# Differential attention: the second value sum in two pieces, and the side work of a unit's nine phases dealt out anew

## The chip, the cores and the metric

The kernel runs on one core of a Trainium2 chip. The engines of that core are named as in the profile: PE multiplies matrices (PEld is its weight load), DVE and POOL work on vectors, ACT computes functions and copies, SP issues DMAs. The metric is the time of one execution on the device in microseconds (us), lower is better. Before the change the median of three runs is 1141.25 us (1139.06 to 1142.85).

## The reference

Four blocks follow one another, each with a layer norm ahead of it and a residual sum behind it: attention A, a mixture of eight small experts, attention B, and the same experts again. The change touches attention A alone. For 2 sequences of 1024 rows of width 512 it computes, cut to its core:

```python
q = rotary((x @ Wq).reshape(b, t, 2 * H, D)); k = rotary((x @ Wk).reshape(b, t, 2 * H, D))   # H = 16, D = 16
v = (x @ Wv).reshape(b, t, H, 2, D)
attn1 = softmax(mask(q1 @ k1.T * scale)) @ concat(v1, v2)      # first map of each head
attn2 = softmax(mask(q2 @ k2.T * scale)) @ concat(v1, v2)      # second map of each head
attn = irfft((rfft(attn1) - lam * rfft(attn2)) * filt)         # along the rows
attn = attn * rsqrt(mean(attn ** 2) + eps) * rms_weight * (1 - LAMBDA_INIT)
out = attn.reshape(b, t, 512) @ Wout
```

The mask is causal. Each head has two score maps that share their values; the second map is taken off the first, weighted by `lam`. The filter along the rows is linear, so it comes after the sum over values.

## The kernel before

Attention A is worked off in 16 units (`NU`): a unit `n` is one sequence and two heads. The 1024 rows of queries are eight tiles of 128, `j` = 0 to 7; because of the mask, tile `j` of queries meets `j + 1` tiles of keys. A unit has nine phases (`NP`), and each phase takes row tiles whose key tiles make up exactly eight: phase 0 is head 0 with tile 7, phase 1 head 1 with tile 7, phase 2 tile 6 of one head and tile 0 of the other, and so on; phase 8 has tile 3 of both heads. Unit `n`'s phase `ph` is step `t = 9 n + ph` of one long loop, whose body writes out the order of instructions for PE, DVE, ACT and POOL by hand. What stands earlier in the body stands earlier in each engine's queue, and every queue is worked off in order.

A row tile goes through three steps `t`, `t + 1`, `t + 2`:

- step `t`, `scores` (L434, its matmuls L475 and L488): PE writes two maps of 128 x 1024 scores; DVE takes the row minimum of each (`minima`, L502 and L510); ACT takes the exponentials and their sums (`exponentials`, L519).
- step `t + 1`, `share` (L539), `divide` (L545, L547) and `join` (L554): POOL and DVE form a ratio from the two sums, and DVE adds the second map times that ratio to the first. The ratio is two small products on POOL: L539 stands at the start of the step, L547 after DVE's reciprocal.
- step `t + 2`, `transpose` (L578, L580): PE turns the joined map in two halves of four blocks each, and ACT copies them to the tile `dt`. A single PSUM bank serves both halves.

Beside this runs the side work. It is entered ahead of time into lists under a step number. The list `large` holds pieces that need the one PSUM bank `misc` of 512 columns: PE's part stands between the two halves of the transposes, and the eviction by ACT or DVE at the end of the step:

- `project` (L355, L366): queries and keys of the next unit, four pieces of 256 columns; pieces 0 and 1 make half 1 (rows 512 to 1023), pieces 2 and 3 make half 0. After the second piece of a half SP issues a DMA that swaps neighbouring rows into `other` (L371).
- `rotate` (L399 to L401), two steps after that second piece, in the list `middle`, which stands after `divide` in the body: three products and sums of 128 x 512 on POOL, and then the DMAs into `keys` (L403) and, for half 1, `swapped` (L408).
- `project_values` (L379, L387): the value tiles of the next pair of units, one or two row tiles at a time; they overwrite those of two pairs before.
- `weigh` (L605, L617, L618): the sum over values. Four groups of matmuls stand side by side in the columns of PE (32 each), one matmul of each group per round. Part 0 has tiles 7, 6 and 0, part 1 has tiles 5 down to 1. ACT evicts it to `oT`.
- `finish` (L627 to L634): PE turns `oT` back, DVE multiplies by the reciprocal sums and writes `result`.
- `spread_half` (L333): the turned input of the second sequence, in the first six units; its layer norm has pieces on DVE, ACT and POOL (`norm_sums`, `norm_tables`, `norm_scale`).

`fold` (L651 to L654) stands in `rear`, the last list of a step: eight sums and differences on POOL that put a unit's result into the form that the filter needs. It comes at phase 6 of the next unit. `bring` loads the second sequence's turned input over the first one's.

Before the change the phases of a unit hold this side work (W0, W1 the two parts of `weigh`, F0, F1 their `finish`, Q0 to Q3 the pieces of `project`, V a value tile, V2 two of them; X, a piece of `spread_half`, only in the first units):

| phase | 0 | 1 | 2 | 3 | 4 | 5 | 6 | 7 | 8 |
|---|---|---|---|---|---|---|---|---|---|
| `large` | Q1 | X, Q2 | W1 | Q3 | F1, V | X, V2 | W0 | F0, V | X, Q0 |
| POOL | | | rotate half 1 | | | rotate half 0 | fold | | |

Units 6 to 9, where the kernel passes from one sequence to the other, have other steps for their value tiles. These lines of the body give the order that matters for POOL: `share` comes early in a step, `divide` and then `middle` in its middle, `rear` last:

```python
if last:
    divide(*last)
do(middle, t)
```

Of the kernel before, what the change touches and what calls it, by code (L numbers as in the profile page):

```python
# [2 lines left out]

# [1 line left out]

# [6 lines left out]
F32 = mybir.dt.float32  # L12
# [6 lines left out]
P = 128  # L19
# [6 lines left out]
NQ = 4  # L26
# [52 lines left out]
def hybrid_layer_kernel(ctx: ExitStack, tc: tile.TileContext, i: dict, out: bass.AP):  # L79
    nc = tc.nc  # L80
# [66 lines left out]
    with ExitStack() as sa:  # L147
# [8 lines left out]
        with ExitStack() as sp:  # L156
# [6 lines left out]
            work = sp.enter_context(tc.tile_pool(name="work", bufs=2))  # L163
# [3 lines left out]
            def misc(name):  # L167
                return ps_m.tile([P, 512], F32, tag="x", name=name)
# [4 lines left out]
            def spare(name):  # L173

                return ps_s.tile([P, 2, 512], F32, tag="s", name=name)[:, 0, :]
# [54 lines left out]
            def load_others(k):  # L230
# [22 lines left out]
                base=0,  # L253
# [172 lines left out]
            NP = len(PHASES)  # L426
            units = [(b, qt, blk) for b in range(NB) for qt in range(NQ) for blk in range(2)]
            NU = len(units)
            least, sums = {}, {}
            weights, turned = {}, {}  # L430
# [133 lines left out]
            def transpose(n, ph, half):  # L564
# [11 lines left out]
                for k in range(4):  # L576
# [4 lines left out]

            PARTS = [
                (0, 3, [[(0, 7, 0)], [(1, 7, 0)], [(0, 6, 0), (0, 0, P)], [(1, 6, 0), (1, 0, P)]]),
                (
                    3,
                    8,
                    [
                        [(0, 5, 0), (0, 3, P)],  # L590
                        [(1, 5, 0), (1, 3, P)],
                        [(0, 4, 0), (0, 2, P), (0, 1, 2 * P)],
                        [(1, 4, 0), (1, 2, P), (1, 1, 2 * P)],
                    ],
                ),
            ]

            def weigh(bank, c0, n, part):
                _, _, groups = PARTS[part]
                po = bank[:, c0 : c0 + P * (part + 2)]  # L600
                order = [[(h, j, c0, k) for h, j, c0 in g for k in range(j + 1)] for g in groups]
                for blocks in zip(*order):
                    for g, (h, j, c0, k) in enumerate(blocks):
                        dt, at = turned[n, h, j, k]
                        nc.tensor.matmul(  # L605
                            po[32 * g : 32 * g + 32, c0 : c0 + P],
                            vals[n // 2 % 2][:, k, 64 * (n % 2) + 32 * h : 64 * (n % 2) + 32 * h + 32],
                            dt[:, at, :],
                            start=(k == 0),
                            stop=(k == j),  # L610
                            tile_position=(0, 32 * g),
                        )
                yield

                full = P * (part + 1)
                oT = work.tile([P, 3 * P], F32, tag="oT", name=f"oT_{n}_{part}")
                nc.scalar.copy(oT[:, 0:full], po[:, 0:full])  # L617
                nc.scalar.copy(oT[64:P, full : full + P], po[64:P, full : full + P])  # L618
                turned[n, part] = oT

            def finish(bank, c0, n, part):
                oT = turned[n, part]
                lo, hi, _ = PARTS[part]
                tp = bank[:, c0 : c0 + 64 * (hi - lo)]
                full = P * (part + 1)
                for at in range(0, full, P):
                    nc.tensor.transpose(tp[:, at : at + P], oT[:, at : at + P], ident)  # L627
                nc.tensor.transpose(tp[:, full : full + 64], oT[64:P, full : full + P], ident[64:P, 64:P])
                yield
                if part == 0:  # L630
                    results[n] = work.tile([P, JT, 64], F32, tag="result", name=f"result_{n}", bufs=1)
                rec = tally.tile([P, 5, 2], F32, tag="rec", name=f"rec_{n}_{part}")[:, 0 : hi - lo, :]
                nc.vector.reciprocal(rec, sums[n][0][:, 2 * lo : 2 * hi].rearrange("p (r h) -> p r h", h=2))
                nc.vector.tensor_mul(  # L634
                    results[n][:, lo:hi, :].rearrange("p r (h f) -> p r h f", h=2),
                    tp.rearrange("p (r h f) -> p r h f", h=2, f=32),
                    rec[:, :, :, None].to_broadcast([P, hi - lo, 2, 32]),
                )
# [21 lines left out]
            front, small, large, middle, final, rear = {}, {}, {}, {}, {}, {}  # L660

            def at(which, t, what, *args):
                which.setdefault(t, []).append((what, args))
# [8 lines left out]

            for n in range(NU):
                t = n * NP
                for part, (t_sum, t_end) in enumerate(((6, 7), (NP + 2, NP + 4 - (n >= NU - 2)))):
                    at(large, t + t_sum, weigh, P * (part + 2), n, part)
                    at(large, t + t_end, finish, (192, 320)[part], n, part)
                at(rear, t + NP + (3 if n == NU - 1 else 6), fold, n)

            PROJECT = (-1, 0, 1, 3)
            VALUES = {p: [(k, w) for k, w in ((-14, 1), (-13, 2), (-11, 1), (-5, 1), (-4, 2), (-2, 1))] for p in range(1, 8)}
            VALUES[4] = [(-5, 1), (-4, 2), (-2, 1), (0, 1), (4, 1), (5, 2)]
            VALUES[5] = [(-11, 1), (-10, 1), (-9, 1), (-8, 1), (-5, 1), (-4, 2), (-2, 1)]

            SPREAD = [n * NP + k for n in range(6) for k in (1, 5, 8)][1:]
            for j in range(JT):
                t = SPREAD[2 * j]
                at(rear, t - 4, load_x, JT + j)  # L690
# [3 lines left out]
                for half in range(2):  # L694
                    at(large, SPREAD[2 * j + half], spread_half, 256, j, half)
            for half in range(2):
                at(rear, (2 * NQ - 2) * NP + PROJECT[3 - 2 * half], bring, half)
            for k in range(4):
                at(rear, 2 * k + (18 if 0 < k < 3 else 0), load_others, k)
            for u in range(2, 2 * NQ):  # L700
# [3 lines left out]
            for u in range(1, NU):  # L704
                t = (u - 1) * NP
                for piece in range(4):
                    if t + PROJECT[piece] >= 0:
                        at(large, t + PROJECT[piece], project, 256, u, piece)
                    if piece % 2:
                        at(middle, t + PROJECT[piece] + 2, rotate, u, 1 - piece // 2)  # L710
                if u % 2 == 0:
                    j = JT
                    for k, w in VALUES[u // 2]:
                        j -= w
                        at(large, u * NP + k, project_values, w * P, u // 2, j, w)
                    assert j == 0
# [89 lines left out]
            t = (NU - 2) * NP  # L806
# [8 lines left out]
            for n in range(MIXED):  # L815
                f = t + FILTER + 1 + n
# [8 lines left out]
            with tc.manual_schedule(engines=ordered | {mybir.EngineType.Pool}):  # L825
# [18 lines left out]
                for t in range(NU * NP + 6):  # L844
# [22 lines left out]
                    if (NU - 1) * NP <= t < (NU - 1) * NP + EC:  # L867
                        part = wout[:, t - (NU - 1) * NP, :]
# [14 lines left out]
                    begun, c0 = [], 0  # L883
                    for what, (width, *args) in large.pop(t, ()):
                        if t >= NU * NP and width == 512:
                            bank, c0 = spare(f"bank_{t}_{len(begun)}"), 0
                        elif c0 == 0:
                            bank = misc(f"bank_{t}")
# [31 lines left out]
        with ExitStack() as sb:  # L920
            wb = sb.enter_context(tc.tile_pool(name="wb", bufs=1, reuse_waits="tile"))
            work = sb.enter_context(tc.tile_pool(name="workb", bufs=2, reuse_waits="tile"))
# [109 lines left out]
            groups, scales, xns, xTs, hidden, acts = {}, {}, {}, {}, {}, {}  # L1032
# [259 lines left out]
            with tc.manual_schedule(engines=ordered):  # L1292
                for t in range(NTILE + 2):
# [28 lines left out]
                    if mixing:  # L1322

                        n = MIXED + t
# [8 lines left out]
                    turned = MIXED + t - 2 if 0 <= t - 2 < NTILE - MIXED else None  # L1333
# [140 lines left out]
```

## Time and profile before

| | us |
|---|---|
| median of three runs | 1141.25 (1139.06 to 1142.85) |
| profiled execution, first to last instruction | 1142.6 |
| attention A's phases, first to last minimum on DVE | 36 to 705 |
| PE busy | 1067.2 (93%) |
| DVE busy | 930.8 (81%) |
| ACT busy | 766.9 (67%) |
| POOL busy | 438.1 (38%) |

Of the profiled execution the page gives the span of its instructions and no other total; the span lies 1.35 us above the median of the runs. A line of a timeline gives start and duration in us, engine, source line, operation, what is written from what, the shape, and in brackets the idle time of the engine before it and what ended that. A line of the table of stretches gives a stretch of the span, its length, each engine's busy time and its number of instructions, the clock that was granted to PE (1.00 is full), and the share and rate of the DMAs. A busy PE is not a PE at its peak, since matmuls overlap.

### The profile page before, as it was taken

How to read it: one execution, taken by the hardware profiler on the slowest of the kernel's cores; microseconds unless marked ns; L12 is line 12 of the kernel's file. 1: busy time of each engine (PE TensorE's matmuls, PEld its weight loads, DVE VectorE, ACT ScalarE, POOL GpSimd, SP SyncE). 2: the span in 40 equal slices, each digit the busy share in tenths (PEclk: the TensorE clock that was granted, in tenths of full speed). 3: DMA queues.
4: the chain of work that ended last, by engine and by line, in shares of the span. 5: the costliest groups of instructions: out<-in, count | busy, mean ns of one | idle time of the engine just before them, and what ended most of it. 6: DMA issues, size and time to landing. Idle time of an engine off the chain costs nothing.

```text
span 1142.6 us, 23491 instructions
## 1 busy us (share of the span) xinstructions
PE 1067.2 (93%) x8680; PEld 732.3 (64%) x8680; DVE 930.8 (81%) x2046; ACT 766.9 (67%) x2010; POOL 438.1 (38%) x689
## 2 busy tenths in 40 slices
PE   6899999999889999999999979889999999999997
PEld 5777777777677877777777655544555455554554
DVE  5699999999889889889989998577787777758677
ACT  3588988989879889899999877243433433443433
POOL 1246446345345444534535672122323223223300
PEclk9999999999989999999999999889999999999999
DMA  5212222211301101110110521200000000001002
GB/s 176 79 42 67 80 80 66 71 38 52 116 15 39 42 16 38 48 33 25 39 43 16 182 114 39 111 1 1 0 1 1 1 1 1 1 1 37 1 19 92
DMA packets 33345, 52.19 MB, mean 46 GB/s; under 512 B 6480, under 2 KB 11088, under 8 KB 33104
## 3 DMA queue, kind: packets, MB, share of 16 engines
q1 hardware_dynamic: 33072, 50.44, 13.8%
q8 instruction: 69, 1.13, 0.4%
q14 instruction: 44, 0.36, 0.1%
q10 hardware_dynamic: 160, 0.26, 0.1%
HBM read 23.42 MB, written 6.29 MB: 26 GB/s over the span
## 4 chain that ended last, share of the span: by engine, by line
PE 55%; DVE 26%; ACT 11%; issue 5%; POOL 2%; DMA 1%; SPq 0%; DVEq 0%; POOLq 0%; ACTq 0%
DVE least L510 8%; PE s L488 8%; ACT p L519 7%; DVE p L554 6%; PE pq_q L1224 5%; PE py L1287 5%; PE bank L355 4%; PE pq_v L1224 4%; PE dtp L578 4%; PE pq_k L1224 4%; PE z L1028 3%; PE bank L605 3%; DVE least L502 3%; PE hr_f L1092 2%; PE y L978 2%
## 5 line engine op out<-in xcount | busy, mean ns | idle before, releaser
L519 ACT ACTIVATE p<-s,least 128x640 f32<-128x640 f32 (+7 forms) x512 | 378.3, 744 | 41.9 <-DVE least L510 27.9
L510 DVE TENSOR_REDUCE least<-s 128x1 f32<-128x896 f32 (+5 forms) x384 | 244.2, 679 | 35.4 <-PE s L488 35.4
L554 DVE SCALAR_TENSOR_TENSOR p<-p,ratio,p 128x1024 f32<-128x1024 f32 (+7 forms) x256 | 227.0, 922 | 3.5 <-POOL ratio L547 3.4
L578 PE MATMUL dtp<-ident,p 128*128 128x128 f32 x1152 | 184.8, 283 | 14.1 <-ACT dt L580 7.9
L580 ACT COPY dt<-dtp 128x512 f32<-128x512 f32 x288 | 168.9, 586 | 42.9 <-PE dtp L578 39.5
L488 PE MATMUL s<-keys,qk 32*128 32x128 f32 (+3 forms) x1408 | 169.0, 445 | 0.0
L578 PEld LDWEIGHTS dtp<-ident,p 128*128 128x128 f32 x1152 | 128.8, 142 | 58.2 <-ACT dt L580 30.4
L502 DVE TENSOR_REDUCE least<-s 128x1 f32<-128x1024 f32 (+1 forms) x96 | 115.9, 1213 | 26.5 <-PE s L488 26.5
L488 PEld LDWEIGHTS s<-keys,qk 32*128 32x128 f32 x1408 | 94.2, 188 | 49.3 <-issue 43.0
L547 POOL TENSOR_TENSOR ratio<-ratio,inverse 128x2 f32<-128x2 f32 (+1 forms) x144 | 28.1, 195 | 243.0 <-DVE inverse L545 217.9
L539 POOL TENSOR_TENSOR ratio<-sums,neg_lam 128x2 f32<-128x2 f32 (+1 forms) x144 | 73.6, 511 | 117.9 <-ACT p L519 117.6
L355 PE MATMUL bank<-xnT,wqk 128*128 128x256 f32 x472 | 115.8, 389 | 2.8 <-ACT raw L366 1.8
L488 PE MATMUL s<-swapped 32*128 32x128 f32 (+2 forms) x896 | 104.8, 345 | 0.0
L519 ACT ACTIVATION_READ_ACCUMULATOR p<-s,least 128x1 f32 x512 | 104.2, 203 | 0.0
L355 PEld LDWEIGHTS bank<-xnT,wqk 128*128 128x128 f32 x472 | 86.0, 192 | 18.0 <-ACT raw L366 5.6
L488 PEld LDWEIGHTS s<-swapped 32*128 32x128 f32 x896 | 71.0, 185 | 9.5
L475 PE MATMUL s<-eye 128*128 128x256 bf16 (+1 forms) x320 | 60.8, 251 | 16.5 <-ACT p L519 15.5
L605 PE MATMUL bank<-dt,v 128*32 128x128 f32 x2304 | 69.5, 274 | 1.7 <-ACT v L387 0.7
L605 PEld LDWEIGHTS bank<-dt,v 128*32 128x32 f32 x2304 | 60.9, 110 | 8.0 <-ACT v L387 4.4
L400 POOL TENSOR_TENSOR other<-other,rope_a_sb 128x512 f32<-128x512 f32 x30 | 63.0, 2099 | 0.0
L1247 POOL TENSOR_TENSOR qkv_v<-qkv_v,qkv_k 128x512 f32<-128x512 f32 x16 | 20.4, 1274 | 108.5 <-DVE qkv_v L1246 107.4
L379 PE MATMUL bank<-wval,xnT 128*128 128x128 f32 x448 | 60.4, 282 | 0.8
(222 smaller groups left out, 1790.8 us busy)
## 6 DMA issues: line engine op xcount, KB each, us to landing
other<-raw SPq DMA_DIRECT2D x64, 128.0 KB, 2.1
xin<-in_query SPq DMA_DIRECT2D x16, 256.0 KB, 2.9
keys<-qk SPq DMA_DIRECT2D x64, 64.0 KB, 1.9
swapped<-keys SPq DMA_DIRECT2D x32, 128.0 KB, 2.3
x_sb<-in_query SPq DMA_DIRECT2D x16, 256.0 KB, 6.3
out_dram<-x_sb SPq DMA_DIRECT2D x16, 256.0 KB, 2.2
swapped<-qk SPq DMA_DIRECT2D x30, 128.0 KB, 2.3
wqk<-in_w_qk SPq DMA_DIRECT2D x8, 256.0 KB, 2.8
```

What stands on the lines that cost most here:

```text
L355: nc.tensor.matmul(pp, wqk[:, part, c, :], xnT[b, half][:, c, t0 : t0 + 256], start=(c == 0), stop=(c == EC - 1),)
L400: engine.tensor_mul(other, other, rope_a[:, 1, cols])
L488: nc.tensor.matmul(s[mm][:, c0 : c0 + w], q[r0 : r0 + 32, j * P - back : (j + 1) * P - back], k[r0 : r0 + 32, s0 - back : s0 - back + w], ...
L502: nc.vector.tensor_reduce(least[n][:, e[0] : e[-1] + 1 : e[-1] - e[0] or 1, mm], s[mm].rearrange("p (g k) -> p g k", g=g), AX.X, ALU.min,)
L510: nc.vector.tensor_reduce(least[n][:, e, mm : mm + 1], s[mm][:, c0 : c0 + w], AX.X, ALU.min)
L519: nc.scalar.activation(ps[mm][:, c0 : c0 + w], sv, AF.Exp, bias=low, scale=-1.0, accum_out=sums[n][mm][:, e : e + 1],)
L539: nc.gpsimd.tensor_mul(ratio[:, w], first, neg_lam.to_broadcast([P, w.stop]))
L554: nc.vector.scalar_tensor_tensor(ps[0][:, c0 : c0 + w], ps[1][:, c0 : c0 + w], ratio[:, k : k + 1], ps[0][:, c0 : c0 + w], ALU.mult, ALU.add,)
L578: nc.tensor.transpose(tp[:, k * P : (k + 1) * P], d[:, c0 : c0 + P], ident)
L580: nc.scalar.copy(dt[:, 4 * half : 4 * half + 4, :], tp.rearrange("p (k q) -> p k q", k=4))
L605: nc.tensor.matmul(po[32 * g : 32 * g + 32, c0 : c0 + P], vals[n // 2 % 2][:, k, 64 * (n % 2) + 32 * h : 64 * (n % 2) + 32 * h + 32], dt[: ...
L1224: nc.tensor.matmul(pq, hTs[n][:, c, :], win(c, s), start=(c == 0), stop=(c == EC - 1))
```

## The change

Part 1 of `weigh` becomes two pieces. Piece 1 has tiles 5 and 4 (groups of six and five rounds), piece 2 has tiles 3, 2 and 1 (four and five rounds). Because groups of a piece are no longer of one length, the rounds are dealt with `zip_longest`, and a group that has ended leaves its place empty. The old part 1 had ten rounds in one step, at phase 2 of the next unit; now piece 1 is at phase 1 and piece 2 at phase 2. Both write into one `oT`, which has its own buffer for each part. Its `finish` moves from phase 4 to 5 (to 4 for unit 13; units 14 and 15 keep phase 3).

The pieces 2 and 3 of `project` move from phases 1 and 3 to phases 3 and 4, and with piece 3 the rotation of half 0 moves from phase 5 to 6; the last unit's projection keeps its old steps. The value tiles move: one at phase 2, one at phase 5 and two at phase 7, in every unit (two at phase 2 of unit 7), so that the irregular steps of units 7 to 9 go away. In the first units the X of phase 5 moves to phase 4, and the layer norm's pieces for it move with it. `bring` of half 0 moves from phase 3 to 4 of unit 6.

| phase | 0 | 1 | 2 | 3 | 4 | 5 | 6 | 7 | 8 |
|---|---|---|---|---|---|---|---|---|---|
| `large` | Q1 | W, piece 1; X | W, piece 2; V | Q2 | X, Q3 | F1, V | W0 | F0, V2 | X, Q0 |
| POOL | | | rotate half 1 | | | | rotate half 0, fold | | |

```diff
-            PARTS = [
-                (0, 3, [[(0, 7, 0)], [(1, 7, 0)], [(0, 6, 0), (0, 0, P)], [(1, 6, 0), (1, 0, P)]]),
-                (
-                    3,
-                    8,
-                    [
-                        [(0, 5, 0), (0, 3, P)],
-                        [(1, 5, 0), (1, 3, P)],
-                        [(0, 4, 0), (0, 2, P), (0, 1, 2 * P)],
-                        [(1, 4, 0), (1, 2, P), (1, 1, 2 * P)],
-                    ],
-                ),
+            PARTS = [(0, 3), (3, 8)]
+            WEIGHED = [
+                (0, 0, True, [[(0, 7, 0)], [(1, 7, 0)], [(0, 6, 0), (0, 0, P)], [(1, 6, 0), (1, 0, P)]]),
+                (1, 0, False, [[(0, 5, 0)], [(1, 5, 0)], [(0, 4, 0)], [(1, 4, 0)]]),
+                (1, P, True, [[(0, 3, 0)], [(1, 3, 0)], [(0, 2, 0), (0, 1, P)], [(1, 2, 0), (1, 1, P)]]),
             ]
...
-                for blocks in zip(*order):
-                    for g, (h, j, c0, k) in enumerate(blocks):
+                for blocks in zip_longest(*order):
+                    for g, block in enumerate(blocks):
+                        if block is None:
+                            continue
+                        h, j, c0, k = block
...
-                full = P * (part + 1)
-                oT = work.tile([P, 3 * P], F32, tag="oT", name=f"oT_{n}_{part}")
-                nc.scalar.copy(oT[:, 0:full], po[:, 0:full])
-                nc.scalar.copy(oT[64:P, full : full + P], po[64:P, full : full + P])
-                turned[n, part] = oT
+                if base == 0:
+                    turned[n, part] = work.tile(
+                        [P, (part + 2) * P], F32, tag=f"oT{part}", name=f"oT_{n}_{part}", bufs=1
+                    )
+                oT = turned[n, part]
+                nc.scalar.copy(oT[:, base : base + P], po[:, 0:P])
+                if half:
+                    nc.scalar.copy(oT[64:P, base + P : base + 2 * P], po[64:P, P : 2 * P])
...
-                for part, (t_sum, t_end) in enumerate(((6, 7), (NP + 2, NP + 4 - (n >= NU - 2)))):
-                    at(large, t + t_sum, weigh, P * (part + 2), n, part)
-                    at(large, t + t_end, finish, (192, 320)[part], n, part)
+                for piece, when in enumerate((6, NP + 1, NP + 2)):
+                    at(large, t + when, weigh, (2, 1, 2)[piece] * P, n, piece)
+                for part, when in enumerate((7, NP + (5 if n < NU - 3 else 4 if n < NU - 2 else 3))):
+                    at(large, t + when, finish, (192, 320)[part], n, part)
                 at(rear, t + NP + (3 if n == NU - 1 else 6), fold, n)
...
-            PROJECT = (-1, 0, 1, 3)
-            VALUES = {p: [(k, w) for k, w in ((-14, 1), (-13, 2), (-11, 1), (-5, 1), (-4, 2), (-2, 1))] for p in range(1, 8)}
-            VALUES[4] = [(-5, 1), (-4, 2), (-2, 1), (0, 1), (4, 1), (5, 2)]
-            VALUES[5] = [(-11, 1), (-10, 1), (-9, 1), (-8, 1), (-5, 1), (-4, 2), (-2, 1)]
-
-            SPREAD = [n * NP + k for n in range(6) for k in (1, 5, 8)][1:]
+            PROJECT = [(-1, 0, 3, 4)] * (NU - 1) + [(-1, 0, 1, 3)]
+            VALUES = {p: [(-16, 1), (-13, 1), (-11, 2), (-7, 1), (-4, 1), (-2, 2)] for p in range(1, 8)}
+            VALUES[4] = [(-13, 1), (-11, 2), (-7, 1), (-7, 1), (-4, 1), (-2, 2)]
+
+            SPREAD = [n * NP + k for n in range(6) for k in (1, 4, 8)][1:]
...
-                    if t + PROJECT[piece] >= 0:
-                        at(large, t + PROJECT[piece], project, 256, u, piece)
+                    when = t + PROJECT[u][piece]
+                    if when >= 0:
+                        at(large, when, project, 256, u, piece)
                     if piece % 2:
-                        at(middle, t + PROJECT[piece] + 2, rotate, u, 1 - piece // 2)
+                        at(middle, when + 2, rotate, u, 1 - piece // 2)
```

## The prediction

> **What bounds the kernel now.** I read the page first (PE is busy 93% of the span, DVE 81%: no engine alone decides), then the phases of one unit as stretches of time, then the timelines of POOL and DVE in the same unit, and last the one unit that is out of line. In the stage that the change touches (36 to 705 us of the span) a unit has nine phases; a phase is taken from its first row minimum on DVE to the next phase's. Units 10 to 13 repeat within 0.02 us, so one stands for all: unit 11, phases 0 to 8 in this order. Columns: length, then busy time (instructions) of PE, PEld, DVE, ACT, POOL, granted clock, DMA share, GB/s.
>
> ```profile
> 494.31:498.69 4.38, 4.23 (x31) 3.23 (x32) 3.74 (x6) 4.24 (x10) 0.78 (x2) 1.00 0.01 4
> 498.69:502.81 4.12, 3.99 (x34) 3.27 (x33) 3.61 (x5) 3.49 (x8) 1.31 (x2) 1.00 0.17 66
> 502.81:507.90 5.09, 4.97 (x108) 4.21 (x108) 4.01 (x6) 4.61 (x14) 3.59 (x3) 1.00 0.01 3
> 507.90:512.22 4.32, 4.16 (x39) 3.34 (x38) 3.87 (x8) 3.69 (x10) 2.47 (x5) 1.00 0.19 54
> 512.22:516.72 4.50, 4.50 (x44) 3.55 (x45) 4.39 (x9) 4.31 (x13) 1.00 (x2) 1.00 0.58 152
> 516.72:521.79 5.07, 4.89 (x54) 3.86 (x55) 5.07 (x8) 4.67 (x15) 3.49 (x4) 1.00 0.01 3
> 521.79:526.09 4.30, 3.97 (x88) 3.06 (x81) 3.93 (x9) 3.37 (x9) 4.02 (x8) 1.00 0.10 34
> 526.09:530.43 4.34, 4.03 (x40) 3.15 (x39) 4.24 (x9) 4.30 (x13) 2.16 (x7) 1.00 0.00 0
> 530.43:534.59 4.16, 4.16 (x31) 3.25 (x31) 3.73 (x7) 3.90 (x12) 0.68 (x2) 1.00 0.00 0
> ```
>
> Light phases stand at 4.12 to 4.38: there a ring sets the length, minimum of map 0 on DVE (1.2), its exponentials on ACT (until 2.4 to 2.7), the next scores on PE (until 4.1 to 4.2), the next minimum. Work beside the ring is free. Three phases stand above it. Phase 2 (5.09) is PE: the second value sum takes 2.39, and the second transposes and the next scores queue behind it. Phase 4 (4.50) carries `finish`, some 0.6 on DVE. Phase 5 (5.07) is DVE without a gap, although its two joins (L554) should take 1.0 and 0.5. The next two answers, POOL's and DVE's timelines of phases 5 to 7 (start, duration, engine, line, operation), say why, and show what POOL's queue holds.
>
> ```profile
> 518.37 1.27 POOL L399 TENSOR_TENSOR raw<-raw,rope_a_sb 128x512 f32<-128x512 f32 x1
> 519.60 1.99 POOL L400 TENSOR_TENSOR other<-other,rope_a_sb 128x512 f32<-128x512 f32 x1
> 521.67 1.34 POOL L401 TENSOR_TENSOR qk<-raw,other 128x512 f32<-128x512 f32 x1
> 522.97 0.19 POOL L539 TENSOR_TENSOR ratio<-sums,neg_lam 128x2 f32<-128x2 f32 x1
> 523.28 0.20 POOL L547 TENSOR_TENSOR ratio<-ratio,inverse 128x2 f32<-128x2 f32 x1
> 523.43 0.46 POOL L651 TENSOR_TENSOR folded<-result 128x128 f32<-128x128 f32 x1
> ...
> 527.06 0.46 POOL L654 TENSOR_TENSOR folded<-result 128x128 f32<-128x128 f32 x1
> 527.47 0.20 POOL L539 TENSOR_TENSOR ratio<-sums,neg_lam 128x2 f32<-128x2 f32 x1
> 527.75 0.20 POOL L547 TENSOR_TENSOR ratio<-ratio,inverse 128x2 f32<-128x2 f32 x1
> ```
> ```profile
> 519.17 2.69 DVE L554 SCALAR_TENSOR_TENSOR p<-p,ratio,p 128x768 f32<-128x768 f32 x2
> ...
> 524.25 1.46 DVE L554 SCALAR_TENSOR_TENSOR p<-p,ratio,p 128x768 f32<-128x768 f32 x2
> ```
>
> The rotation's three products fill POOL from 518.37 to 523.01, and the same pair of joins takes 2.69 beside them against 1.46 a phase later: the two engines block each other. Then come share and ratio of phase 6, the fold until 527.5, share and ratio of phase 7 (until 527.95). The joins of phases 6 and 7 start at 524.25 and 528.55, so both ratios are in time, the second by 0.6 us. What a late one costs is seen once, in unit 6, where the rotation starts 2.9 us late (its DMA landed late): POOL, DVE, and the granted clock in the phase after (seventh figure).
>
> ```profile
> 313.99 1.28 POOL L399 TENSOR_TENSOR raw<-raw,rope_a_sb 128x512 f32<-128x512 f32 x1 [2.89 <-DMA other<-raw]
> ```
> ```profile
> 318.31 1.78 DVE L554 SCALAR_TENSOR_TENSOR p<-p,ratio,p 128x768 f32<-128x768 f32 x2 [2.09 <-POOL ratio L547]
> ```
> ```profile
> 320.00:325.40 5.40, 4.38 (x30) 3.10 (x29) 4.42 (x10) 3.86 (x10) 3.24 (x9) 0.57 0.00 0
> ```
>
> DVE idles 2.09 for the ratio, and phases 6, 7 and 8 of that unit last 6.34, 5.39 and 5.05 against 4.30, 4.34 and 4.16.
>
> **The change part by part**, for a unit like 11; units 1 to 13 have the new order.
>
> *Rotation of half 0: phase 5 to 6* (pieces 2 and 3 go from phases 1 and 3 to 3 and 4; the rotation follows two phases later). Its DMA `other` still has two phases, and the two key DMAs that SP issues after it still land some seven microseconds before phase 0 reads them, so those cost nothing. On POOL it now stands directly ahead of the fold, which stays at the end of phase 6. Behind both, in order, wait share and ratio of phase 7; behind the ratio waits DVE's join, and behind that `finish` 0 and phase 8's minima. From the start of phase 6: ratio of phase 6 done at 1.64 (as 518.37 − 516.72); rotation 4.65 beside the joins, as in the old phase 5, to 6.29; DVE's joins end at 5.07, as there, so phase 6 grows from 4.30 to 5.07. The fold took 4.03, of which one operation of 1.04 instead of 0.32 is the joins' doing; DVE will stand still, so 3.3, to 9.6. Share and ratio: 0.48 more to join start (527.47 to 527.95): 10.08. Before, that join began at 528.55 − 521.79 = 6.76. Loss 3.32 per unit: 0.77 in phase 6, 2.55 in phase 7. Ends: rotation 3.86 (unit 6, 313.99 to 317.85, no joins beside it) and fold 3.3 give 9.3, a loss of 2.5; rotation 4.65 and fold 4.03 give 10.8, a loss of 4.1. I take 3.32, since phase 6 has the old phase 5's joins and phase 7 none until the ratio is there.
>
> *Value tiles, two in phase 7 rather than one.* PE gets 0.88 more (eight passes at 0.11). Then scores(8) end at about 5.1 of phase 7 instead of 4.24: hidden under the 6.9 that DVE now needs; if that cover went, 0.85. PE then waits only from 5.1 to the first join's end at 5.01 + 0.88 = 5.9.
>
> *Phase 5: value tiles of width two and the rotation leave, `finish` 1 and one value tile come.* That is the old phase 4's content with the same minima, so 4.50: −0.56 (ends −0.4, −0.77, the floor of 4.30).
>
> *Phase 4: `finish` and value tile leave, a projection comes:* the old phase 3's content: 4.31, −0.19 (ends 0, −0.3).
>
> *The sum in two.* Old: ten rounds of four matmuls, each 0.22 (two passes of 0.11), 2.2. New: six rounds in phase 1 (the last two only half filled), five in phase 2: 11 rounds, 0.22 more. Phase 1 had a projection of 1.9 in that place, now 1.3: the ring keeps it at 4.12. One more eviction (0.29) per unit meets ACT at 3.49 busy of 4.12 there: nothing; if ACT were full, 0.3. In phase 2 five rounds and a value tile, 1.1 + 0.9 + 0.1 for the switch, replace 2.2 and its 0.1: −0.19 (ends 0, and −0.78 if it reached the ring's 4.31). The split frees PE in phase 2, but the value tile fills most of it.
>
> Per unit: 3.32 − 0.56 − 0.19 − 0.19 − 0.04 (phase 8) = +2.34; 13 units: +30.4. Corrections: units 1 to 4 already had normalisation on DVE in phase 7 (4.88 and 5.35), which the wait partly covers: −1.0. Units 7 to 9 lose their irregular value tiles: 5.27 to 4.38, 5.05 to 4.16, 5.11 to 4.38, 5.00 to 4.12, −3.4; phase 2 of unit 7 gets two tiles and that of unit 9 was 4.77 already, +1.5. Unit 14 has a projection and the first sum in phase 1 (+1.3) and only five rounds in phase 2 (−0.8); the sums at the end of unit 15 shorten the tail by 0.5; unit 0: +0.1. Together +27.6. Unit 6 repeats its late DMA in either kernel. The profiled span is 1142.6, so 1170.2; it lies 1.35 above the runs' median of 1141.25, on which I put the sum: **1169**.
>
> **A rule against a row.** In unit 6 PE stood idle 1.63 (318.01 to 319.64) and the clock was granted at 0.57 in the phase after, which with the next lost 1.9; idle times of 1.06 at 108 and 193 us left it at 1.00. So where PE idles 0.8, I count no clock loss, and 1.9 per unit if the wait comes out long. The Trainium skill, "TensorE: Matmul & The Clock Gate", section "Why this matters for your kernels", wants idle gaps under about 3 us, one idle window bringing half clock. By it no unit would lose its clock and the sum stays at 1169 even at the upper end; by unit 6's row it would be up to 1194.
>
> **The rivals.**
> *Stall and clock (1194).* If scores(8) end nearer 4.2 than 5.1, or POOL takes the upper end, PE idles over 1.6 and phases 7 and 8 lose 1.04 + 0.89 more, 13 times: +25. For it: unit 6. Against: the second value tile keeps PE busy.
> *No stall (1147).* POOL gets through in time, for instance because its spans are rough; then remain 0.77 in phase 6 and 0.85 in phase 7 (PE, tile two) against gains of 0.98: +0.64, 13 times, less 2.8 of corrections: +6. Against: 4.65 and 3.3 of work are in order ahead of the ratio with 4.3 to 5.1 of phase to hold them.
> *Faster (1128).* Phase 2 falls to the ring's 4.31: −0.78 rather than −0.19, with 0.75 from phases 4 and 5, −1.5 per unit; it decides as soon as the POOL group costs under 1.5 instead of 3.3. With 0.6, 13 × −0.9 less 1.5 is −13. Against: both end values of that group lie above 2.5.
> *The change doesn't do what it says:* the split relieves no phase since the tile takes its place; +0.19 × 13 = 2.5 on the forecast, inside its range.
>
> **How the numbers follow.** Forecast 0.68, its own range by the POOL bounds 13 × (−0.8, +0.8): 1159 to 1179. Stall and clock 0.13, no stall 0.12, faster 0.05, rest 0.02. The range 1154 to 1187 leaves out the faster case, most of no stall, and the clock case where nearly all units lose it. About 0.3% (3.4 us) is what a measurement here can tell. Slower: 0.68 + 0.13 + 0.11 = 0.92; same 0.03; faster 0.05.
>
> **What would show it.** In the new profile POOL must run L400 to L402 and the fold without a ratio between them in phase 6; DVE's join of phase 7 must idle some 2.5 for POOL's ratio in each of units 1 to 13; phase 6 about 5.1 with joins of some 2.7, phase 7 about 6.9, phase 5 about 4.5, phase 4 4.3, phase 2 4.9. Clock at 1.00 in phases 7 and 8 speaks for the forecast, 0.5 for the first rival. I am wrong if the fold takes well under 3 us when DVE is still, or if PE turns out to set phase 7.

## The result, and the profile after

The changed kernel takes 1189.79 us in the median of four runs (1180.98 to 1195.0) against 1140.44 before (the three runs of the first table and a fourth): a ratio of 1.0414, 95% interval 1.0364 to 1.0465. It is slower, as forecast, but by 49 us and not by 28. The profiled run took 1187.56 with a span of 1185.2. First the page of the changed kernel: the chain of work that ended last, by engine, and the group of the joins (busy us, mean ns, then the idle time before them and who ended most of it).

```profile
PE 54%; DVE 19%; ACT 12%; POOL 10%; issue 4%; DMA 1%; POOLq 0%; DVEq 0%; SPq 0%; ACTq 0%
...
L555 DVE SCALAR_TENSOR_TENSOR p<-p,ratio,p 128x1024 f32<-128x1024 f32 (+7 forms) x256 | 228.4, 927 | 30.5 <-POOL ratio L548 30.2
```

POOL, 2% of the chain before, now has 10%, and DVE's wait for POOL's ratio has gone from 3.4 to 30.2 us. The same unit as in the forecast, unit 11, phases 0 to 8 (length, busy time of PE, PEld, DVE, ACT, POOL, granted clock, DMA share, GB/s):

```profile
528.48:532.52 4.04, 3.97 (x30) 3.06 (x29) 3.73 (x5) 3.62 (x8) 0.78 (x2) 1.00 0.01 2
532.52:536.83 4.31, 4.05 (x71) 3.22 (x72) 3.61 (x5) 3.84 (x9) 1.19 (x2) 1.00 0.16 61
536.83:541.58 4.75, 4.75 (x72) 3.99 (x73) 3.99 (x6) 4.06 (x12) 3.25 (x3) 1.00 0.02 3
541.58:546.05 4.47, 4.36 (x40) 3.51 (x40) 3.87 (x8) 4.25 (x13) 2.77 (x5) 1.00 0.15 45
546.05:550.36 4.31, 4.31 (x39) 3.46 (x39) 3.86 (x7) 3.97 (x12) 1.00 (x2) 1.00 0.48 105
550.36:554.87 4.51, 4.44 (x40) 3.23 (x41) 4.40 (x10) 4.31 (x13) 0.87 (x2) 1.00 0.17 62
554.87:559.94 5.07, 4.78 (x94) 3.55 (x92) 5.07 (x8) 4.65 (x15) 3.50 (x4) 1.00 0.00 0
559.94:566.73 6.79, 4.88 (x46) 4.02 (x46) 4.32 (x10) 3.82 (x10) 4.62 (x12) 1.00 0.06 22
566.73:572.65 5.92, 5.38 (x27) 4.11 (x28) 3.73 (x6) 4.21 (x12) 0.68 (x2) 0.71 0.00 0
```

Phases 4 and 5 are shorter, 6 and 7 longer, and then there is a line that the forecast did not have: phase 8, 5.92 instead of 4.16, with the clock at 0.71. The timelines of POOL, DVE and PE across phases 6 to 8 (start, duration, engine, line, operation, and in brackets the idle time before and who ended it):

```profile
559.82 1.33 POOL L402 TENSOR_TENSOR qk<-raw,other 128x512 f32<-128x512 f32 x1
561.11 0.45 POOL L651 TENSOR_TENSOR folded<-result 128x128 f32<-128x128 f32 x1
...
564.34 0.19 POOL L540 TENSOR_TENSOR ratio<-sums,neg_lam 128x2 f32<-128x2 f32 x1
564.61 0.19 POOL L548 TENSOR_TENSOR ratio<-ratio,inverse 128x2 f32<-128x2 f32 x1
```
```profile
557.32 2.70 DVE L555 SCALAR_TENSOR_TENSOR p<-p,ratio,p 128x768 f32<-128x768 f32 x2
...
564.84 1.41 DVE L555 SCALAR_TENSOR_TENSOR p<-p,ratio,p 128x640 f32<-128x640 f32 x2 [2.36 <-POOL ratio L548]
```
```profile
563.03 1.16 PE L489 MATMUL s<-keys,qk 32*128 32x384 f32 x16
565.87 0.63 PE L579 MATMUL dtp<-ident,p 128*128 128x128 f32 x4 [1.68 <-DVE p L555]
567.27 3.25 PE L356 MATMUL bank<-xnT,wqk 128*128 128x256 f32 x8 [0.78 <-ACT v L388]
```

POOL goes from the rotation straight into the fold, and the ratio ends at 564.8, 9.9 us after the start of the phase 6 in which that group began. DVE stands still for 2.36; PE, with its scores done at 564.2, stands still for 1.68 and, for a bank, 0.78 more. The projection behind that takes 3.25. In the kernel before it took 1.99:

```profile
530.89 1.99 PE L355 MATMUL bank<-xnT,wqk 128*128 128x256 f32 x8
```

The clock has been halved: 0.71 is the mean over phase 8, and in the stretch from 567.85 to 571.27 it is 0.50 (last section).

### The profile page after: what moved, and what is told of

Read it like the earlier page. It is cut to its first block, busy times and chain, and to the rows that moved or that the text cites. A ratio compares the mean times of both kernels' runs of the same rounds, so it can differ in the third digit from the quotient of the medians.

```text
span 1185.2 us, 23494 instructions
## 1 busy us (share of the span) xinstructions
PE 1083.9 (91%) x8680; PEld 743.1 (63%) x8680; DVE 933.9 (79%) x2046; ACT 768.4 (65%) x2025; POOL 428.8 (36%) x689
## 4 chain that ended last, share of the span: by engine, by line
PE 54%; DVE 19%; ACT 12%; POOL 10%; issue 4%; DMA 1%; POOLq 0%; DVEq 0%; SPq 0%; ACTq 0%
PE bank L356 8%; ACT p L520 7%; PE s L489 6%; DVE least L511 6%; PE dtp L579 4%; PE py L1288 4%; PE pq_q L1225 4%; PE pq_v L1225 4%; DVE p L555 4%; PE pq_k L1225 4%; PE z L1029 3%; POOL other L401 2%; PE hr_f L1093 2%; DVE least L503 2%; PE bank L602 2%
## 5 line engine op out<-in xcount | busy, mean ns | idle before, releaser
L555 DVE SCALAR_TENSOR_TENSOR p<-p,ratio,p 128x1024 f32<-128x1024 f32 (+7 forms) x256 | 228.4, 927 | 30.5 <-POOL ratio L548 30.2
L579 PEld LDWEIGHTS dtp<-ident,p 128*128 128x128 f32 x1152 | 131.5, 143 | 79.0 <-issue 29.4
L356 PE MATMUL bank<-xnT,wqk 128*128 128x256 f32 x472 | 132.1, 429 | 9.9 <-ACT v L388 8.2
L356 PEld LDWEIGHTS bank<-xnT,wqk 128*128 128x128 f32 x472 | 94.7, 211 | 31.7 <-ACT v L388 13.9
L602 PE MATMUL bank<-dt,v 128*32 128x128 f32 x2304 | 76.1, 275 | 2.4 <-ACT oT L617 0.8
L476 PE MATMUL s<-eye 128*128 128x256 bf16 (+1 forms) x320 | 56.4, 253 | 12.5 <-ACT p L520 12.2
```

The costliest lines, as they stand in the source:

```text
L356: nc.tensor.matmul(pp, wqk[:, part, c, :], xnT[b, half][:, c, t0 : t0 + 256], start=(c == 0), stop=(c == EC - 1),)
L555: nc.vector.scalar_tensor_tensor(ps[0][:, c0 : c0 + w], ps[1][:, c0 : c0 + w], ratio[:, k : k + 1], ps[0][:, c0 : c0 + w], ALU.mult, ALU.add,)
L579: nc.tensor.transpose(tp[:, k * P : (k + 1) * P], d[:, c0 : c0 + P], ident)
L602: nc.tensor.matmul(po[32 * g : 32 * g + 32, c0 : c0 + P], vals[n // 2 % 2][:, k, 64 * (n % 2) + 32 * h : 64 * (n % 2) + 32 * h + 32], dt[: ...
```

## The experiments

Theory Q: the rotation of half 0 and the fold, now together in POOL's queue, make the ratio of phase 7 late; PE starves and loses its clock. Rival S: the newly dealt side work on PE itself makes phases 7 and 8 long. Rival W: the divided sum costs. The intervals are those of the ratio to the kernel before on the same chip.

### The fold taken out of the rotation's way

```diff
-                at(rear, t + NP + (3 if n == NU - 1 else 6), fold, n)
+                at(rear, t + NP + (3 if n == NU - 1 else 8), fold, n)
-                if part == 0:
-                    results[n] = work.tile([P, JT, 64], F32, tag="result", name=f"result_{n}", bufs=1)
+                results[n, part] = work.tile(
+                    [P, hi - lo, 64], F32, tag=f"result{part}", name=f"result{part}_{n}", bufs=2 - part
+                )
```

The lines are cut to their core: `finish` and `fold` also write and read the two tiles instead of one.

> The changed kernel with the fold moved from phase 6 to phase 8 (the first three row tiles of a result get a second buffer, since the next unit's finish 0 comes first). Theory Q (POOL's queue): the rotation of half 0 and the fold stand together ahead of the ratio of phase 7, which comes 2.4 us late, and PE, left idle, loses half its clock in phase 8. Then here DVE no longer idles for the ratio in phase 7, phase 7 falls from 6.79 to 4.4 to 4.7, phase 8 from 5.9 to 4.2 with the clock at 1.00, phase 6 stays at 5.07; a unit of some 40.2 and a total of 1133 to 1143. Rival S (the side work itself: two value tiles and finish 0 on PE make phase 7 long): phases 7 and 8 stay above 10 together, total over 1165. Rival W (the divided sum costs): total over 1165.

Measured: 1143.29 us, 0.3 above the range of theory Q, ratio 1.0014 (0.9999 to 1.0028). Unit 11, phases 6, 7 and 8:

```profile
518.00:523.07 5.07, 4.77 (x95) 3.55 (x92) 5.07 (x8) 4.65 (x15) 3.50 (x4) 1.00 0.01 3
523.07:527.40 4.33, 4.33 (x43) 3.75 (x44) 4.22 (x10) 3.57 (x9) 2.09 (x4) 1.00 0.08 30
527.40:531.66 4.26, 4.21 (x31) 3.22 (x31) 3.86 (x6) 4.10 (x12) 2.66 (x6) 1.00 0.00 0
```

POOL's timeline has the ratio of phase 7 right behind the rotation, and DVE's join no longer waits for it:

```profile
522.94 1.33 POOL L402 TENSOR_TENSOR qk<-raw,other 128x512 f32<-128x512 f32 x1
524.23 0.19 POOL L540 TENSOR_TENSOR ratio<-sums,neg_lam 128x2 f32<-128x2 f32 x1
524.56 0.19 POOL L548 TENSOR_TENSOR ratio<-ratio,inverse 128x2 f32<-128x2 f32 x1
```
```profile
525.52 1.40 DVE L555 SCALAR_TENSOR_TENSOR p<-p,ratio,p 128x640 f32<-128x640 f32 x2
```

The whole loss is gone, with all the new side work in its place: phase 7 is 4.33 with two value tiles, so S and W both fall as its cause. Some 46 us stand against the place of eight small POOL operations. The rest of the change then gains nothing: the nine phases sum to 40.29, against 40.28 before.

### The fold's place in the kernel before (control)

The same edit in the kernel before.

> The kernel before with the fold at phase 8 instead of 6 (and the second buffer for three row tiles), a control for the first experiment. Theory Q: in the kernel before, the ratio of phase 7 was in time already, so nothing changes: 1137 to 1146. If the fold's place in phases 6 and 7 costs in itself (it shares POOL and memory ports with DVE's joins), this is faster than before by more than 4 us, and the first experiment's return is due to that and not to the order of the queue.

Measured: 1140.96 us, ratio 0.9996 (0.998 to 1.0013). The fold costs nothing at phase 6 that this interval shows, as long as no rotation stands directly ahead of it. So the return above is due to the order in the queue, and not to the second buffer, which this kernel has as well.

### The rotation alone

```diff
-                        at(middle, t + PROJECT[piece] + 2, rotate, u, 1 - piece // 2)
+                        at(middle, t + PROJECT[piece] + 2 + (piece == 3 and u < NU - 1), rotate, u, 1 - piece // 2)
```

> The kernel before, with nothing changed but the rotation of half 0, which comes one phase later (phase 6) in units 0 to 13. Theory Q: phase 6 grows to 5.07, phase 7 to some 6.8 with DVE idle 2.4 for POOL's ratio, phase 5 falls to 4.4 to 4.9; with the lost clock in phase 8 the total is 1175 to 1200. Rivals S and W: the side work on PE and the sum are as before, so the total stays within 1136 to 1146.

Measured: 1187.86 us, ratio 1.0416 (1.0392 to 1.044): the whole loss from one line in the kernel before. Phases 5, 6 and 7 of unit 11, and DVE's join in phase 7:

```profile
553.57:557.90 4.33, 4.22 (x42) 3.43 (x41) 3.86 (x9) 3.94 (x11) 0.87 (x2) 1.00 0.01 4
557.90:562.98 5.08, 4.94 (x95) 3.71 (x94) 5.08 (x8) 4.82 (x16) 3.50 (x4) 1.00 0.01 3
562.98:569.76 6.78, 4.15 (x38) 3.17 (x38) 4.32 (x10) 3.82 (x10) 4.61 (x12) 1.00 0.05 19
```
```profile
567.87 1.41 DVE L554 SCALAR_TENSOR_TENSOR p<-p,ratio,p 128x640 f32<-128x640 f32 x2 [2.36 <-POOL ratio L547]
```

The wait of 2.36 and the 6.78 of phase 7 are those of the changed kernel to 0.01. The 5.07 of a phase follows the rotation: phase 5 drops to 4.33 without it, though PE still has two value tiles there, and phase 6 takes it on. PE in phase 7, with a single value tile, waits twice:

```profile
565.78 0.33 PE L475 MATMUL s<-eye 128*128 128x128 bf16 x3 [0.70 <-ACT p L519]
566.04 1.16 PE L488 MATMUL s<-keys,qk 32*128 32x384 f32 x16
568.90 0.63 PE L578 MATMUL dtp<-ident,p 128*128 128x128 f32 x4 [1.70 <-DVE p L554]
```

It waits 0.70 for ACT's exponentials before the scores, has the scores done 4.22 into the phase, and then waits 1.70 for the late join.

### PE kept busy during the wait

```diff
                 tp = turning(f"dtp_{n}_{ph}_{half}")
+                if ph == 6 and half == 0 and 1 <= n <= 13:
+                    for k in range(10):
+                        nc.tensor.matmul(
+                            tp[:, 0 : 3 * P], eye[:, 0, :], eye.rearrange("p k q -> p (k q)"), start=True, stop=True
+                        )
```

> The changed kernel with ten more matmuls per unit (128x384, bfloat16, results never read) on PE ahead of the transposes that wait for the late join, in units 1 to 13. If the granted clock is what makes phase 8 last 5.9 (theory Q with its second half): clock 1.00 in phase 8, phase 7 unchanged at 6.8, phase 8 at 4.1 to 4.4, total 1166 to 1174 in spite of the added work. If the clock is a bystander, and phase 8 is long because its projection waits for its bank: phase 8 at 5.9 or more, total 1186 to 1200.

Measured: 1174.65 us, 0.7 above the range, ratio 1.0308 (1.0289 to 1.0327): 15 us faster than the changed kernel, by adding work. Phases 7 and 8 of unit 11:

```profile
546.83:553.63 6.80, 6.51 (x56) 4.92 (x56) 4.32 (x10) 3.82 (x10) 4.62 (x12) 1.00 0.07 22
553.63:557.87 4.24, 3.69 (x27) 2.94 (x28) 3.73 (x6) 3.85 (x10) 0.68 (x2) 1.00 0.00 0
```

The late ratio is still there (6.80), the clock is full, and phase 8 is back at 4.24. The changed kernel shows the same without any filling: its unit 13 has the same two idle times of PE (1.67 and 0.77), kept the clock, and its phase 8 lasts 4.24. So the loss has two parts: the wait itself, and the clock that the idle PE loses. From the first to the last phase of attention A the kernel before takes 668.5, this one 698.4, the changed one 713.9 in its profiled run: 29.9 for all but the clock, 15.5 for the clock.

### Less filling

The same with `range(4)`.

> The changed kernel with four filler matmuls per unit instead of ten, so that PE still idles some 1.0 and 0.8 us around phase 8. If any idle time of over 1 us costs the clock: as the changed kernel, 1182 to 1195. If it takes a stretch of 3.4 us in which PE is busy less than about half (as the windows of the earlier runs suggest: 0.47 and less ahead of each drop in attention A, 0.54 and more where none came): few drops, phase 8 mostly at 4.2, total 1168 to 1180.

Measured: 1182.21 us, ratio 1.0355 (1.0331 to 1.0379): between the changed kernel and the full filling, and at the lower edge of the first alternative's range. Phase 8 is 4.1 to 4.5 in six of the 13 units and 5.9 to 6.1 in seven. The first alternative was not tested: with four matmuls PE idles 0.81 to 0.84 twice in units 5 to 13, never over 1 us, and six of these nine units lost the clock all the same, while unit 13 of the changed kernel kept it with 1.67. So the length of one idle time does not decide. My "few drops" was wrong too. Two stretches of 3.41 us with the idle times, in units 9 and 2, each with the next one (third figure from the end: the clock):

```profile
471.82:475.23 3.41, 1.76 (x10) 1.08 (x9) 3.02 (x7) 0.86 (x2) 0.34 (x2) 1.00 0.00 0
475.23:478.64 3.41, 3.41 (x13) 2.55 (x11) 2.49 (x4) 2.19 (x7) 0.68 (x2) 0.50 0.00 0
161.21:164.62 3.41, 1.77 (x10) 1.46 (x11) 3.24 (x8) 0.86 (x2) 0.00 (x0) 1.00 0.00 0
164.62:168.03 3.41, 2.86 (x24) 2.02 (x24) 3.08 (x5) 2.81 (x8) 0.68 (x2) 1.00 0.31 77
```

PE was busy for 1.76 and 1.77 of them, a share of 0.52; the first lost the clock and the second did not. The border lies near one half here and is not sharp in this measure. The bounds in my expectation were already too narrow for the runs before it: in the changed kernel 0.48 kept the clock, and with the rotation alone 0.50 lost it in four units and kept it in one.

### The divided sum alone

```diff
+                for piece, when in enumerate((6, NP + (1 if 5 <= n < NU - 2 else 2), NP + 2)):
+                    at(large, t + when, weigh, (2, 1, 2)[piece] * P, n, piece)
+                for part, when in enumerate((7, NP + 4 - (n >= NU - 2))):
+                    at(large, t + when, finish, (192, 320)[part], n, part)
```

Beside these lines the kernel before takes over the change's dividing of `weigh` and nothing else.

> The kernel before with the second sum divided in two (piece 1 at phase 1, piece 2 at phase 2) for units 5 to 13 and nothing else moved, so that phase 1 holds piece 1 beside its projection. Theory Q: phase 1 grows from 4.12 to some 5.3, phase 2 falls from 5.09 to 4.3, 0.3 to 0.5 more per unit, total 1141 to 1147. Rival W (dividing the sum costs in itself, by its rounds that are half filled and its eviction): over 1 us per unit, total over 1150.

Measured: 1154.23 us, ratio 1.0123 (1.0103 to 1.0142). Phases 1 to 3 of unit 11, and PE in phases 1 and 2:

```profile
504.32:510.07 5.75, 5.75 (x80) 4.74 (x80) 3.61 (x5) 4.11 (x9) 1.30 (x2) 1.00 0.13 48
510.07:514.35 4.28, 3.74 (x62) 2.75 (x61) 4.00 (x7) 3.54 (x9) 2.78 (x3) 1.00 0.00 0
514.35:519.01 4.66, 4.52 (x40) 3.69 (x41) 3.96 (x7) 4.62 (x15) 3.44 (x5) 1.00 0.09 31
```
```profile
504.77 1.50 PE L602 MATMUL bank<-dt,v 128*32 128x128 f32 x44
...
510.46 1.30 PE L602 MATMUL bank<-dt,v 128*32 128x128 f32 x36
...
512.89 0.27 PE L476 MATMUL s<-eye 128*128 128x256 bf16 x1 [0.43 <-ACT p L520]
```

1.16 more per unit (41.44 against 40.28), where I expected 0.3 to 0.5. The two pieces take 1.50 and 1.30 for the 2.39 of the whole, 0.41 more on PE; phase 1 takes the first in full (+1.63), but phase 2 gives back only 0.81, because it meets the ring: PE waits 0.43 for ACT's exponentials. Phase 3 is 0.34 longer. By the numbers this is W's (over 1 per unit, the total over 1150). But the changed kernel takes the projection out of phase 1, where the experiment leaves it, and with the fold moved its phase 1 is 4.07 and its unit 40.29: there the divided sum is not what costs.

### A try at a version that beats both

The first experiment's kernel with the value tile of phase 2 in phase 6:

```diff
-            VALUES = {p: [(-16, 1), (-13, 1), (-11, 2), (-7, 1), (-4, 1), (-2, 2)] for p in range(1, 8)}
-            VALUES[4] = [(-13, 1), (-11, 2), (-7, 1), (-7, 1), (-4, 1), (-2, 2)]
+            VALUES = {p: [(-13, 1), (-12, 1), (-11, 2), (-4, 1), (-3, 1), (-2, 2)] for p in range(1, 8)}
```

> The first experiment's kernel with the value tile of phase 2 moved to phase 6, where DVE and POOL set the length (5.07) and PE waits, for all pairs of units alike. If PE alone sets phase 2 with its five rounds and the tile (5.0), phase 2 falls to the ring's 4.3, phase 6 stays between 5.07 and 5.4, a unit of 39.6 to 39.9 and a total of 1131 to 1138, faster than both kernels. If phase 6 has no room for it: phase 6 at 5.7 or more, total 1141 to 1150.

Measured: 1145.49 us, ratio 1.0035 (1.0022 to 1.0048). Phases 2, 6 and 7 of unit 11:

```profile
500.68:505.06 4.38, 3.94 (x62) 2.95 (x62) 4.00 (x7) 3.80 (x11) 2.88 (x3) 1.00 0.01 4
...
518.54:523.88 5.34, 5.24 (x100) 4.25 (x98) 5.14 (x8) 4.54 (x14) 3.77 (x4) 1.00 0.01 3
523.88:528.74 4.86, 4.80 (x47) 3.98 (x47) 4.33 (x10) 4.58 (x13) 1.82 (x4) 1.00 0.07 27
```

Phase 2 falls by 0.61 as expected and phase 6 grows by 0.27, but phase 7 grows by 0.53: the room that PE had in phase 6 had been used already. In the first experiment `finish` 0 starts with phase 7 (523.07), and that head start holds the second tile; here it starts 0.52 into it (524.40). A unit is 40.61: phase 6 came out as in the first case, the total as in the second. No version here beats the kernel before.

## Why the prediction was right or wrong

| phase of unit 11 | before | forecast | changed | changed, PE kept busy |
|---|---|---|---|---|
| 2 | 5.09 | 4.90 | 4.75 | 4.99 |
| 4 | 4.50 | 4.31 | 4.31 | 4.46 |
| 5 | 5.07 | 4.50 | 4.51 | 4.51 |
| 6 | 4.30 | 5.07 | 5.07 | 5.07 |
| 7 | 4.34 | 6.89 | 6.79 | 6.80 |
| 8 | 4.16 | 4.12 | 5.92 | 4.24 |
| unit | 40.28 | 42.62 | 44.17 | 42.75 |

- *Rotation of half 0, phase 5 to 6.* Right in mechanism and size: the ratio of phase 7 ends 9.9 after the start of phase 6 and the join starts at 10.0 (10.08 forecast), phase 6 is 5.07, the wait 2.36. The fold beside a still DVE took 3.23 (561.11 to 564.34; 3.3 forecast). Two experiments show the cause from both sides.
- *Value tiles, two in phase 7.* This step failed, and with it the clock, which it let me count as nothing. I let scores(8) end at 5.1 of phase 7 and PE wait 0.8; they end at 4.25 and PE waits 1.68. While DVE stretches phase 6, PE and ACT run ahead: `finish` 0 starts at −0.01 of phase 7 instead of 0.77. With one tile (the rotation alone) PE spends 0.70 of this head start waiting for ACT and ends the scores at 4.22 all the same; the second tile fills that wait instead of moving the scores. I also left out that the projection of phase 8 waits for the bank, 0.78.
- *The clock.* So the condition of the first rival ("if scores(8) end nearer 4.2 than 5.1") was met in units 1 to 13, and that rival had the right mechanism; its 1194 was nearer than 1169. Its size was too large: it counted 1.93 in each of 13 units, 25 in all, and by the runs with and without filling the clock cost 15.5. It fell in phase 8 of units 2 to 12. In unit 11 phase 8 loses 1.68 by it, and a part comes back: the phases 0 to 4 are together 0.25 shorter than with full clock (0, 2 and 4 shorter, 1 and 3 longer).
- *Rule against row.* The row was right in 11 of 13 units. The rule of the Trainium skill that I weighed ("TensorE: Matmul & The Clock Gate", section "Why this matters for your kernels") would have kept the clock full at 1.68 and 0.78 of idle time; the runs show it halved, so the measurement decides.
- *Phase 4, phase 5, phase 2.* Phase 5 right (−0.56). Phases 2 and 4 are −0.34 and −0.19 in the changed kernel, but −0.10 and −0.04 in the one with PE kept busy; forecast −0.19 each. The two pieces of the sum take 1.50 and 1.30, not 1.3 and 1.1.
- *Corrections.* "Unit 6 repeats its late DMA in either kernel" was wrong: its phase 7 is 6.79 like those of units 5 to 13, so 3.5 of the forecast were not lost there; units 1 to 5 lost 2.5 more than I gave them. The sum of all steps without the clock was 27.6; measured with PE kept busy it is 29.9.
- *The range.* 1187 left out the case in which nearly all units lose their clock, which is the one that came. Neither of the two signs of being wrong that I had named appeared: they asked about the fold and about PE setting phase 7, not about how long PE idles. Two slips in the working changed little: the upper end of the POOL group (10.8) is a loss of 4.0 and not 4.1, and at that end the sum without a clock loss would be some 1179, not 1169. The other rivals: no stall, the faster case and the change without effect are out. What is left without the stall, with the fold moved, is 1143, near the 1147 of the second rival, and for a reason it did not have: phase 7 holds two tiles without 0.85 more.

Of the 20.8 between forecast and median, 15.5 is the clock and 2.3 the sum of the steps; the last 3 are of the size of the spread between runs and were not settled.

## What to carry to other kernels

When an operation is moved, write down for the engine that gets it what stands directly behind it in its queue, and who waits there: here two blocks that were each harmless met, and a product of two columns behind them stopped three engines (DVE for 2.36, PE for 1.68, ACT for up to 2.3). A PE that waits may cost a second time (15.5 of some 45 us here), so look in the profile for a spot with a like gap and read its granted clock before setting the price of a wait. And a phase that is stretched by one engine is a head start for the others, which hides work one phase later and uncovers a wait: work out anew when each engine starts the next phase before counting on added work to keep it busy.

## What the runs showed of the hardware

The clock was granted in stretches of 3.41 us on a fixed grid. In each of the nine traces it stands at 1.00 or 0.50, every piece at 0.50 lasts one or two times 3.413 us (but for a last one at the end of the trace), and each begins a whole number of 3.413 after the one before; in the changed kernel those of units 10, 11 and 12 begin at 523.48, 567.85 and 612.23, 13 stretches apart. The table of stretches of the changed kernel on that grid, in units 11 and 13, each time the stretch with the idle time and the next:

```profile
564.44:567.85 3.41, 1.21 (x7) 0.95 (x8) 2.91 (x5) 0.94 (x3) 0.43 (x3) 1.00 0.00 0
567.85:571.27 3.42, 3.42 (x12) 2.69 (x11) 2.61 (x5) 2.12 (x6) 0.68 (x2) 0.50 0.00 0
653.19:656.60 3.41, 1.65 (x9) 1.34 (x10) 3.31 (x7) 1.18 (x3) 0.19 (x2) 1.00 0.00 0
656.60:660.01 3.41, 3.32 (x28) 2.43 (x27) 2.90 (x4) 3.41 (x11) 0.54 (x2) 1.00 0.00 0
```

PE was busy for 1.21 of the stretch in unit 11 (0.35; in unit 12 for 1.41, 0.41) and got 0.50 in the next; with 1.65 in unit 13 (0.48) it kept 1.00. The same two idle times of 1.68 and 0.78 (within 0.01) lay in all three units; only where the grid cut them differed. In units 1 to 13 of the nine traces a stretch at full clock with a share of 0.47 or less was followed by half clock each time, and one of 0.53 or more never; in between it went both ways. In unit 15 of five traces a share of 0.67 lost the clock too, so the busy time of PE is not all that counts, and what else does is open. A unit of 44.17 is nearly 13 such stretches (44.4), so the grid creeps by 0.2 per unit, and nearly every unit is hit in the same place until one falls out. That also goes with the spread of the changed kernel's runs: 1180.98, 1187.56, 1192.02 and 1195.0 had mean granted clocks of 0.984, 0.976, 0.970 and 0.966. That the start of the grid relative to the kernel makes this difference was not tried.
